# A recurrence of 576 steps before the main loop: its matrix products, and the products of zeros between them, split over TensorE's four column groups

## The chip, the cores and the metric

The kernel runs on one core of a Trainium2 chip. The metric is the device time of one execution in microseconds (us). The engines are named as in the profile: PE is TensorE's products, PEld TensorE's weight loads (they overlap the products), DVE is VectorE, ACT is ScalarE, POOL is GpSimd, SP is the engine that issues most transfers. L683 is line 683 of the kernel before.

## What is computed

The input x has 4 images of 128 channels and 64 x 64 pixels. Four layers follow one another, each with a residual sum: an attention over neighbourhoods of 7 x 7 with sampled offsets; a recurrent layer; eight layers of a selective state-space model; and a mixture of 64 experts. The change touches the second. Cut to what matters, the reference there is:

```python
Wx = einsum('bti,hi->bth', x, W)            # then normalised over all b and t, times gamma, plus beta
def step(yt, wx_t):
    yt = sigmoid(wx_t + yt @ V.T)
    return yt, yt
_, ys = scan(step, zeros((B, H)), swapaxes(Wx, 0, 1))
```

B is 4, H is 128, and there are 4096 steps (the pixels of an image). Each step needs the one before it, so the steps are a chain: a product of the 128 x 128 matrix V with four columns, a sum, a sigmoid.

## The kernel before

**The stages.** `tile_kernel` calls `conv_layer` (the attention and the product with W, whose result goes to HBM as wx_d), makes a `Recurrence`, calls `mamba` (the state-space layers) and then `experts`. All order is written out by hand: instructions run on each engine in the order in which the program gives them.

**The recurrence.** `Recurrence.step(t)` and `Recurrence.tanh(t)` do one step for all four images. The sigmoid is computed as a tanh, with the constants folded into V (`vt`, halved) and into the input. Steps come in blocks of RT = 64. At the first step of a block, L678 puts the block's input, 64 x 4 columns, into a PSUM tile `p` by a product with the identity; each step then adds its product with `vt` into its own four columns of that tile (L683, `start=False`), and ACT takes the tanh of those four columns (L691) into `z`, which is the moving operand of the next step's product. `vt` is the stationary operand, so TensorE loads it as weights. The matrices are f32. In the middle of a block `load` fetches the next block's input (L664, L666) and ACT scales it (L667); at a block's end POOL makes y from z and adds x1 (L697, L698), and SP writes the result to HBM (L700).

**The lead.** The state-space layers work on chunks of 512 pixels, so they can begin when the recurrence is ahead by somewhat more than a chunk. `mamba` therefore runs the first PRE = 512 + 64 = 576 steps by themselves, in a loop of their own: `rec.step(t)`, one or two calls of `rec.busy`, `rec.tanh(t)`. The other 3520 steps are given out one by one between the instructions of the state-space layers, by the list STEPS.

**The products of zeros.** `rec.busy(out, n)` (L655) multiplies a 128 x 128 bf16 tile of zeros, `still`, with n x 128 columns of the same zeros, into a PSUM tile `idle` that nobody reads. It does no part of the computation; it keeps TensorE working. In the lead each step has one with n = NB = 4 (512 columns), and every second step one more with n = 2 (256 columns). They stand on TensorE behind the step's product and ahead of the next step's.

**Where column groups are used already.** A product with 32 columns of weights writes 32 of the 128 partitions of PSUM, and the four possible positions are the array's four column groups. The kernel has such products at L433 in the attention and at L1423, L1508 and L1543 in the experts: in each, four products that follow one another in the program go to the four groups.

Of the kernel before, what the change touches and what calls it, by code (L numbers as in the profile page):

```python
# [20 lines left out]
P = 128  # L21
# [25 lines left out]
TL = 512  # L47
# [562 lines left out]
class Recurrence:  # L610
# [56 lines left out]
        nc.scalar.activation(wx, wx, AF.Identity, scale=self.sc, bias=self.sh)  # L667
        self.got[n] = wx, x1

    def step(self, t):  # L670

        nc = self.nc
        n, k = divmod(t, RT)
        if k == 0:

            self.wx, self.x1 = self.got.pop(n)
            self.p = self.ps.tile([P, RT, B], F32, tag="p", name="p")
            nc.tensor.matmul(  # L678
                self.p, self.ops.ident, self.wx.rearrange("p b t -> p t b"), start=True, stop=False,
                skip_group_check=True,  # L680
            )
            self.z = self.w.tile([P, RT, B], F32, tag="z", name="z")
        nc.tensor.matmul(  # L683
            self.p[:, k, :], self.vt, self.before, start=False, stop=True, skip_group_check=True
        )

    def tanh(self, t):

# [58 lines left out]
def mamba(tc, ops, I, rec, x2_d, x3_d):  # L747
# [8 lines left out]
    nc = tc.nc  # L756
    NSLOT = NS // 2 * NH
    NB = TL // P
# [5 lines left out]
    with ExitStack() as ctx:  # L764
# [408 lines left out]
        def get(i):  # L1173
            return bodies[i] if 0 <= i < len(bodies) else None
# [34 lines left out]
        load(0)  # L1209
        idle = psf.tile([P, TL], F32, tag="f0", name="idle")  # L1210
        for t in range(PRE):
            rec.step(t)
            rec.busy(idle, NB)
            if t % 2:
                rec.busy(idle, NB // 2)
            rec.tanh(t)
        for s in bodies[0:3]:
            for what in ("fetch", "mean", "var", "rv", "rr", "first"):
# [2 lines left out]
        t = PRE  # L1221
        for i in range(-2, len(bodies) + 1):
            o, n, q = get(i), get(i + 1), get(i - 1)
# [364 lines left out]
@with_exitstack  # L1588
def tile_kernel(ctx: ExitStack, tc: tile.TileContext, I, out):
    nc = tc.nc  # L1590
    const = ctx.enter_context(tc.tile_pool(name="const", bufs=1))
    dram = ctx.enter_context(tc.tile_pool(name="scratch", bufs=1, space=DRAM))
    nc.scalar.preload_act_table_set(EXP_LN)
    ops = Ops(nc, const)
    stats = const.tile([P, B * NBLK, 6], F32, name="stats")
    gating_w = gating_weights(tc, const, ops, I)
    x1_d = dram.tile([P, B, L], F32, name="x1_d")
    x2_d = dram.tile([P, B, L], F32, name="x2_d")
    x3_d = dram.tile([P, B, L], F32, name="x3_d")
    wx_d = dram.tile([P, B, L], F32, name="wx_d")  # L1600

    with tc.manual_schedule():
        with ExitStack() as c:
            conv_layer(tc, ops, I, x1_d, wx_d, stats)
            rec = Recurrence(c, tc, ops, I, stats, wx_d, x1_d, x2_d)
            mamba(tc, ops, I, rec, x2_d, x3_d)
        experts(tc, ops, I, gating_w, x3_d, out)
# [90 lines left out]
```

## Time and profile before

| | us |
|---|---|
| median of three runs (14884.57 to 14900.8) | 14895.22 |
| the profiled execution | 14892.08 |
| its span, first to last instruction | 14890.3 |
| the lead's tanh, first to last start | 1506.0 to 1881.6 |
| PE busy over the span | 14160.7 (95%) |
| DVE busy | 12974.0 (87%) |
| POOL busy | 12589.8 (85%) |
| ACT busy | 10980.2 (74%) |

The profile is of one execution, 1.8 us longer than its span. The granted clock of TensorE was 0.984 of full speed on average; the trace lists it by stretches, and in the lead it was 1.00 throughout. A busy PE in this profile is not PE at its peak, since products are pipelined and their ends are modelled: PE is shown busy for 361.7 of the 370 us from 1510 to 1880, although it streams for less than half of that time. A product or a load is recorded with the time at which it starts; two loads of which the second starts before the first is over are no error of the view.

In the groups' lines, the first number after the bar is busy time in us, then comes the mean duration of one in ns, and after the second bar the idle time of the engine just before them and what ended it. `128*32 128x128` in a product's line means weights of 128 rows and 32 columns, and a moving operand of 128 partitions and 128 elements.

### The profile page before, as it was taken

The numbers are of one execution on the slowest core, as the hardware profiler recorded it, in microseconds if no ns is written. First come the engines' busy times: TensorE is split into PE (matmuls) and PEld (weight loads), VectorE is DVE, ScalarE is ACT, GpSimd is POOL, SyncE is SP. The second block draws the span as 40 slices with busy tenths as digits, with TensorE's granted clock in tenths as the row PEclk, the third lists the DMA queues.
The fourth block names the chain that finished last, engine by engine and source line by source line (L and its number), as shares of the span: only waits on it lengthen the run. The fifth ranks groups of instructions, "written<-read, shape, count | busy, mean of one in ns | idle before, by whom it ended". The sixth has DMA issues, their size and how long they took to land. (4 is left out here: it accounts for less than half of the span.)

```text
span 14890.3 us, 307789 instructions
## 1 busy us (share of the span) xinstructions
PE 14160.7 (95%) x124378; PEld 10821.2 (73%) x124378; DVE 12974.0 (87%) x16043; ACT 10980.2 (74%) x21400; POOL 12589.8 (85%) x5760
## 2 busy tenths in 40 slices
PE   7999989999999999999999999999999999999996
PEld 3444467777777777777777777777777777777775
DVE  8997079998999899999998999989999999989994
ACT  6887267777777777777777777777777777777773
POOL 5564079999999999999999999999999999999993
PEclk8999999999999999999999999999999999999998
DMA  0000034434443434343444344344434343434344
GB/s 23 26 26 23 29 122 144 144 136 148 142 147 135 152 137 150 132 151 138 149 142 144 137 149 142 138 145 145 146 136 151 138 149 133 154 131 145 133 146 184
DMA packets 600044, 1914.56 MB, mean 129 GB/s; under 512 B 347488, under 2 KB 347872, under 8 KB 434272
## 3 DMA queue, kind: packets, MB, share of 16 engines
q1 hardware_dynamic: 598480, 1894.60, 36.1%
q8 instruction: 984, 16.12, 0.4%
q14 instruction: 436, 3.57, 0.1%
q10 hardware_dynamic: 144, 0.26, 0.0%
HBM read 1823.10 MB, written 71.57 MB: 127 GB/s over the span
## 5 line engine op out<-in xcount | busy, mean ns | idle before, releaser
L1100 POOL TENSOR_TENSOR hs<-hs,Cb 128x2048 f32<-128x2048 f32 x2048 | 9300.9, 4543 | 749.0 <-DVE state L1092 562.3
L1075 DVE TENSOR_TENSOR_SCAN hs<-dA,state,dBx 128x512 f32<-128x512 f32 x7168 | 8808.2, 1267 | 700.2 <-PE dBx L1042 561.3
L1020 ACT ACTIVATE dA<-dt,A 128x512 f32<-128x512 f32 x7168 | 4730.4, 716 | 11.6 <-DVE hs L1075 5.5
L1104 PE MATMUL yT<-ident,hs 128*128 128x128 f32 x32768 | 4376.9, 277 | 30.4 <-POOL hs L1100 30.2
L1042 PE MATMUL dBx<-diag,dtxT 64*128 64x128 f32 x57344 | 4195.3, 283 | 27.1 <-DVE hs L1075 20.1
L1104 PEld LDWEIGHTS yT<-ident,hs 128*128 128x128 f32 x32768 | 3785.4, 147 | 433.6 <-issue 349.2
L1042 PEld LDWEIGHTS dBx<-diag,dtxT 64*128 64x128 f32 x57344 | 3509.4, 187 | 800.7 <-issue 741.3
L683 PEld LDWEIGHTS p<-z,vt 128*128 128x128 f32 x8192 | 1283.9, 189 | 881.8 <-ACT z L691 401.8
L691 ACT ACTIVATE z<-p 128x4 f32<-128x4 f32 x4096 | 702.3, 171 | 1396.6 <-PE p L683 1368.8
L683 PE MATMUL p<-z,vt 128*128 128x4 f32 x8192 | 1453.7, 248 | 107.1 <-ACT z L691 98.4
L1075 DVE TENSOR_TENSOR_SCAN hs<-dAp,state,hs 128x512 f32<-128x512 f32 x1024 | 1273.3, 1273 | 296.7 <-POOL hs L1063 296.7
L1063 POOL TENSOR_TENSOR hs<-Bb,dtx 128x512 f32<-128x512 f32 x1024 | 1284.9, 1280 | 0.0
L904 DVE SCALAR_TENSOR_TENSOR xc<-f,taps,xc 128x511 f32<-128x511 f32 (+2 forms) x1536 | 1115.8, 726 | 53.4 <-ACT z L691 49.3
L1020 ACT ACTIVATE dAp<-dt,A 128x512 f32<-128x512 f32 x1024 | 708.8, 692 | 491.6 <-DVE hs L1075 470.1
L279 DVE SCALAR_TENSOR_TENSOR acc<-qp,dww,acc 128x512 f32<-128x512 f32 x1184 | 892.4, 754 | 25.6
L979 POOL TENSOR_TENSOR dtx<-dt,xc 128x512 f32<-128x512 f32 x512 | 651.6, 1273 | 217.5 <-ACT dt L973 217.5
L293 POOL TENSOR_TENSOR off<-off,to 128x512 f32<-128x512 f32 x288 | 366.4, 1272 | 412.7 <-ACT to L291 400.0
L1020 ACT ACT_TABLE_LOAD x511 | 655.6, 1283 | 9.0
L898 ACT ACTIVATE xc<-f,taps 128x512 f32<-128x512 f32 x512 | 350.7, 685 | 414.7 <-PE f L895 281.1
L919 PE MATMUL f<-u,given 128*128 128x512 f32 x1024 | 600.6, 670 | 3.8 <-DVE xc L904 3.8
L847 PEld LDWEIGHTS f<-avg,sq 128*128 128x128 f32 x2048 | 257.0, 197 | 466.0 <-ACT sq L1148 466.0
L895 PE MATMUL f<-u,given 128*128 128x512 f32 x1024 | 567.0, 636 | 0.8 <-DVE u L868 0.8
(235 smaller groups left out, 15160.8 us busy)
## 6 DMA issues: line engine op xcount, KB each, us to landing
Cb<-c_d SPq DMA_DIRECT2D x1024, 1024.0 KB, 7.2
diag<-spare SPq DMA_DIRECT2D x256, 1792.0 KB, 8.8
Bb<-c_d SPq DMA_DIRECT2D x256, 512.0 KB, 4.8
given<-in_m_given_dram SPq DMA_DIRECT2D x64, 640.0 KB, 8.6
slab<-in_w_dram SPq DMA_DIRECT2D x60, 512.0 KB, 9.9
x<-x_d SPq DMA_DIRECT2D x96, 256.0 KB, 3.0
c_d<-dbl SPq DMA_DIRECT2D x512, 32.0 KB, 1.6
x_d<-x SPq DMA_DIRECT2D x63, 256.0 KB, 3.2
```

Source lines behind the costliest of these rows:

```text
L279: nc.vector.scalar_tensor_tensor(rows(to), x, dww[:, t : t + 1], rows(o.acc), ALU.mult, ALU.add)
L683: nc.tensor.matmul(self.p[:, k, :], self.vt, self.before, start=False, stop=True, skip_group_check=True)
L691: nc.scalar.activation(self.z[:, k, :], self.p[:, k, :], AF.Tanh, scale=0.5)
L904: nc.vector.scalar_tensor_tensor(x, o.v[h][:, : TL - k], taps[:, o.l, h, DC - 1 - k : DC - k], x, ALU.mult, ALU.add)
L919: nc.tensor.matmul(o.pz[h], o.given[:, at : at + P], o.u, start=True, stop=True)
L979: nc.gpsimd.tensor_tensor(to, blocks(o.dt[h]), blocks(o.xc[:, h, :]), ALU.mult)
L1020: nc.scalar.activation(o.dA[j][:, k, :], o.dt[h], AF.Exp, scale=A[:, o.l, h, n : n + 1])
L1042: nc.tensor.matmul(o.dBx[j][:, at : at + 64, :], o.dtxT[h][row, n, :], o.diag[row, n, :, 2 * sp : 2 * sp + 2], start=True, stop=True,)
L1063: nc.gpsimd.tensor_tensor(hs[:, k, :].rearrange("p (q n t) -> p q n t", n=NB, q=2), o.Bb[:, k, :].rearrange("p (q n t) -> p q n t", n=NB, ...
L1075: nc.vector.tensor_tensor_scan(hs[:, k, :], o.dA[j][:, k, :], hs[:, k, :] if sp == SP_B else o.dBx[j][:, :, k], state[:, o.l, o.b, h, s : ...
L1100: nc.gpsimd.tensor_tensor(hs, hs, o.Cb[f], ALU.mult)
L1104: nc.tensor.matmul(o.yT[:, n, :], x[:, n * P : (n + 1) * P], ops.ident, start=start and n == 0, stop=True, is_transpose=True, skip_group_c ...
```

## The change

In the lead, `step(t, 4)` gives four products in place of one: each takes 32 columns of `vt` as weights, the same four columns of z as the moving operand, and writes 32 partitions of `p`. The product with the identity at the start of a block (L678) stays whole. In place of `rec.busy` stands `busy_tiles`: four products of zeros with 512 columns each, with 32 columns of weights each, one for each column group; the additional 256 columns of every second step are left out. The steps outside the lead call `step(t)` with one tile, which is one product as before.

```diff
+    def busy_tiles(self, out):
+
+        for j in range(0, P, 32):
+            self.nc.tensor.matmul(
+                out[j : j + 32, :].rearrange("p (n t) -> p n t", n=TL // P), self.still[:, j : j + 32],
+                self.still.unsqueeze(1).to_broadcast([P, TL // P, P]), start=True, stop=True,
+            )
+
-    def step(self, t):
+    def step(self, t, tiles=1):
...
-        nc.tensor.matmul(
-            self.p[:, k, :], self.vt, self.before, start=False, stop=True, skip_group_check=True
-        )
+        m = P // tiles
+        for j in range(0, P, m):
+            nc.tensor.matmul(
+                self.p[j : j + m, k, :], self.vt[:, j : j + m], self.before, start=False, stop=True,
+                skip_group_check=True,
+            )
...
         for t in range(PRE):
-            rec.step(t)
-            rec.busy(idle, NB)
-            if t % 2:
-                rec.busy(idle, NB // 2)
+            rec.step(t, 4)
+            rec.busy_tiles(idle)
             rec.tanh(t)
```

In the order of the built instructions, a step of the lead has on TensorE four products, of which the first waits for ACT, and then four times a load of zeros and its product; before, it had one product that waits for ACT, and one or two times a load of zeros and its product. The other engines have the same instructions in the same order as before.

## The prediction

> **What bounds the kernel now.** I began with the page's busy shares by slice. In slice 5 (1489 to 1861 us) VectorE and GpSimd are all but idle, so whatever is running there runs alone. The list of waits of 1510 to 1880 us says what it is:
>
> ```profile
> engine line waited for: us in total, times, longest us
> ACT z L691 <- PE p L683: 269.2, 551, 1.4
> PEld p L683 <- ACT z L691: 176.3, 552, 0.4
> ```
>
> TensorE (PE; its weight loads are the row PEld) and ScalarE (ACT) wait for each other, about 550 times. This is a chain of steps with nothing beside it: a shorter step ends the stage sooner. The chain that ended last does not show it, because that view's pieces cover only the last 300 us. From the same stretch, the groups kept apart by shape (busy us, mean ns | idle before):
>
> ```profile
> L683 PE MATMUL p<-z,vt 128*128 128x4 f32 x1120 | 215.0, 262 | 8.3
> L683 PEld LDWEIGHTS p<-z,vt 128*128 128x128 f32 x1120 | 167.4, 188 | 179.9 <-ACT z L691 176.3 <-issue 3.6
> L655 PEld LDWEIGHTS <-still 128*128 128x128 bf16 x840 | 108.7, 153 | 0.0
> L691 ACT ACTIVATE z<-p 128x4 f32<-128x4 f32 x560 | 96.9, 173 | 269.2 <-PE p L683 269.2
> ```
>
> 560 tanh but 1120 loads and products: each f32 product is two passes, each with a weight load of its own. The timeline of one step:
>
> ```profile
> 1601.38 0.30 PEld L683 LDWEIGHTS p<-z,vt 128*128 128x128 f32 x2 [0.33 <-ACT z L691]
> 1601.38 0.39 PE L683 MATMUL p<-z,vt 128*128 128x4 f32 x2
> 1601.51 0.21 PEld L655 LDWEIGHTS <-still 128*128 128x128 bf16 x2
> 1601.62 0.48 PE L655 MATMUL idle<-still 128*128 128x512 bf16 x2
> 1601.80 0.17 ACT L691 ACTIVATE z<-p 128x4 f32<-128x4 f32 x1 [0.48 <-PE p L683]
> 1602.03 0.19 PEld L683 LDWEIGHTS p<-z,vt 128*128 128x128 f32 x1 [0.30 <-ACT z L691]
> ```
>
> A step takes 1602.03 - 1601.38 = 0.65 us; over the trace's single records it is 648 ns. Those records of a step, counted from its first load: second load at 108 ns, so one load of 128 columns takes about 107; second product at 134; zeros' product at 246; tanh from 423 to 596; next load at 648. A second load that starts at 108 is done at 215, and only then can the second product stream its 4 columns. So the step is 215 ns of loads, 208 from there to the tanh, 173 of tanh and 52 to the next load: 648. A third of it is loading weights that never change. The zeros stream from 246 to 460 (512 columns, 214 ns), in every second step to 567: they end 80 ns or more before the next load, off the path.
>
> **What four column groups cost here.** The kernel already has such products at L1423: 128 columns stream, each product with 32 columns of weights. The first loads and products of one burst, from the timeline:
>
> ```profile
> 14786.25 0.16 PEld L1423 LDWEIGHTS pp<-slab,pk 128*32 128x32 f32 x8 [0.17 <-issue]
> 14786.25 0.32 PE L1423 MATMUL pp<-slab,pk 128*32 128x128 f32 x4
> ```
>
> And windows over such bursts and over L1543's, which are of the same kind (busy us and count of PE, PEld, DVE, ACT, POOL, then the granted clock, which the trace lists in steps of 3.41 us):
>
> ```profile
> 14786.20:14794.20 8.00, 8.00 (x203) 6.45 (x205) 5.48 (x10) 2.26 (x4) 3.30 (x1) 1.00 0.01 3
> 14812.62:14816.03 3.41, 2.23 (x48) 1.19 (x38) 0.00 (x0) 0.00 (x0) 0.00 (x0) 1.00 1.03 419
> 14816.03:14819.45 3.42, 1.52 (x35) 0.95 (x33) 0.00 (x0) 0.00 (x0) 0.00 (x0) 1.00 1.02 413
> 14819.45:14822.86 3.41, 2.90 (x52) 2.31 (x56) 0.00 (x0) 0.00 (x0) 0.00 (x0) 0.50 1.03 420
> ```
>
> In the burst eight loads fit into 0.16 us: single records start at 0, 7, 14, 20 ns for the first pass and 29, 35, 42, 49 for the second. So a load of 32 columns takes 27 to 29 ns, and the groups follow one another at 7, side by side. The second pass's products start 133 ns after the first's: 107 of streaming and those 27.
>
> **Part 1, the step's products.** By these times the last group's second load starts at 49 and is done at 76, where it was 215: 139 ns less. What follows (208, 173, 52) stays, so the tanh starts at 284 and the next load at 509. PRE is 576 steps; in nine of them the new block's L678 comes first, its two products of 256 columns hide V's loads, and I count no gain. 567 x 139 ns = 79 us.
>
> A rule of the Trainium skill speaks against this. "TensorE: Matmul & The Clock Gate", section Back-to-back issue gap, puts a floor of about 25 ns from one product's start to the next, however few columns it has. Eight products of 4 columns would need 27 + 7 x 25 = 202 ns, 13 less than now and not 139, worth 7 us in all. The row has four products start within 0.32 - 0.30 = 0.02 us, 7 ns apart, when they lie in different column groups. I take the row, but its products are long: that short ones of one group also keep the pace is not shown.
>
> **Part 2, the zeros.** Per step one product of 512 columns, in every second step another of 256, becomes four of 512 with 32 columns of weights, one for each group. They are queued behind the step's products on TensorE and run while the tanh is awaited. Their loads come behind the products', so they can start at about 105 to 125 ns. From below: all four stream at once, 213 ns, ending near 340, 170 before the next load: nothing on the path. From above: bf16 groups take turns, 4 x 216 = 864 ns, ending near 967. No bf16 product in column groups is in the trace. The nearest row is L1508, f32, 512 columns, 32 columns of weights: its groups of four start 7 ns apart and repeat every 429 ns, which is also what one pass of an unsplit 512-column f32 product takes. I take the first. If the cover is gone, each ns of zeros beyond 509 - 105 = 404 costs one ns per step.
>
> **Part 3, instructions.** The build has 12 instructions per step on TensorE where there were 4 on average; in the trace's records, 8 loads and 8 products and 4 of each for zeros, 24 in 509 ns: 21 ns each. In the window at 14786 us above, 203 + 205 = 408 ran in 8.00 us, 19.6 each, in spite of waits for VectorE, for longer than any short queue could hide. I count nothing; were 27 ns the limit the step would be 648 again.
>
> **Part 4, the clock.** The zeros are what keeps TensorE busy enough for the full clock (1.00 all through this stage). Now they and the step's products stream (213 + 53 + 7) / 648 = 42% of the time; after, counted once for four groups, (213 + 7) / 509 = 43%, and the staggered starts add to it. The last three windows above show how column groups count: 48 products of 107 ns, four at a time, are 38% of a window, and the next was still granted 1.00; 35 products are 27%, and the next was granted 0.50. So I count nothing. At half clock (L1423's rounds of four take 213 ns there, 109 at full clock) the zeros would take 427 ns, the step some 575: still 73 below now.
>
> Changing between split and unsplit products at the nine L678 costs between nothing and one draining product (0.27 us) each way: 0 to 5 us. I take 0. No wait, DMA or other engine's work is added; the first of four products carries the wait for ACT, and behind it are only its own group.
>
> **Sum.** The profiled execution took 14892.1 us (span 14890.3). 14892.1 - 79 = 14813; the median of the runs is 3 us above it, so 14816 there.
>
> **The rivals.** (a) *The gain is halved.* If each of the four products reports its end by itself, the same skill page (section The cost: per-tile semaphore tail) has 26 ns for each: 3 x 26 = 79 off 139, 60 left, 34 us, 14861. Half clock gives about the same: 73 x 567 = 41, 14854. For it: no such short groups are in the trace. (b) *It hardly does what it says.* Short products in groups keep the 25 ns floor, or the instructions the 27: 0 to 7 us, 14890. Against it: the 7 ns starts and 19.6 ns above. (c) *Slower: the zeros take turns.* Products end at 105, zeros at 967, and the next step's products wait behind them on TensorE: 967 per step, 319 x 567 = 181 us more, 15076. It decides from 545 ns of zeros on (648 - 103), two and a half products in turn; two pairs in turn (432) would still gain. Against it: L1508's groups, whose f32 pass reads as many bytes per ns as bf16 does. For it: the zeros are loads and products written out singly, which no split product of the trace is.
>
> **How the numbers follow.** The gain as computed 0.62; halved (a) 0.13; hardly any (b) 0.08; slower, (c) or any mixture of it, 0.17. The range goes from 14795, where the tail behind the second product also shrinks by 35 ns, through (a) to (b)'s 14890; only (c) is left out. A measurement of this kernel can tell some 0.2% (30 us) from no change: faster 0.75, same 0.08, slower 0.17.
>
> **What would show it.** Right: tanh starts about 509 ns apart; loads of 128x32 at L693's products, eight starting within 50 ns; the zeros of four groups starting together and over before the next load; the stage from 1505 to 1886 us ending near 1807; the clock 1.00 in it; all later stages as long as before. Wrong: a tanh interval of 570 to 590 with clock 0.5 or with late tanh starts (a); zeros' starts 216 ns apart (c); loads of V that idle on "issue" (b).

## The result, and the profile after

| us | before | changed |
|---|---|---|
| median of 5 runs each | 14892.51 | 14829.48 |
| the profiled execution | 14892.08 | 14829.05 |
| its span | 14890.3 | 14827.2 |
| the lead, first to last tanh | 1506.0 to 1886.1: 380.1 | 1505.3 to 1826.1: 320.8 |

The ratio is 0.996, with a 95% interval from 0.9945 to 0.9974: 63 us less, where 79 were forecast. One number given earlier has to be corrected: the table ahead of the prediction ends the lead before at 1881.6 us. That counted seven semaphore records of ACT as tanh; the last of the 576 starts at 1886.1, which is what the prediction itself used.

The lead is 59.3 us shorter, it begins 0.7 us sooner, and the remaining 3 us lie in the 13 ms behind it, which is within what executions of one kernel differ by (the five of the changed kernel go from 14828.4 to 14838.2).

In the list of waits of 1510 to 1820 us the pair is the same as before. TensorE waits no less for each tanh, but ACT waits far less for the products:

```profile
ACT z L702 <- PE p L693: 210.5, 546, 1.5
PEld p L693 <- ACT z L702: 199.7, 547, 1.2
PEld p L693 <- issue: 6.7, 9, 0.8
```

210.5 us in 546 waits are 0.39 us each, where it was 0.49. The third line is new in this size: eight of its nine cases, 6.0 us, are the starts of blocks, where split loads now stand behind a whole product, and the ninth is a pause that comes up below. The groups by shape, from 1510 to 1800 us:

```profile
L673 PE MATMUL idle<-still 128*32 128x512 bf16 x2072 | 207.4, 381 | 0.0
L693 PE MATMUL p<-z,vt 128*32 128x4 f32 x4152 | 128.0, 183 | 31.0 <-ACT z L702 0.9 <-issue 0.6
L702 ACT ACTIVATE z<-p 128x4 f32<-128x4 f32 x518 | 89.5, 173 | 197.3 <-PE p L693 197.3
L693 PEld LDWEIGHTS p<-z,vt 128*32 128x32 f32 x4147 | 82.3, 108 | 193.0 <-ACT z L702 186.3 <-issue 6.7
```

Eight loads and eight products of 32 columns for each tanh, and four products of zeros. The tanh takes 173 ns as before. The timeline of one step:

```profile
1600.41 0.16 PEld L693 LDWEIGHTS p<-z,vt 128*32 128x32 f32 x8 [0.36 <-ACT z L702]
1600.41 0.24 PE L693 MATMUL p<-z,vt 128*32 128x4 f32 x8
1600.46 0.12 PEld L673 LDWEIGHTS <-still 128*32 128x32 bf16 x4
1600.49 0.40 PE L673 MATMUL idle<-still 128*32 128x512 bf16 x4
1600.72 0.17 ACT L702 ACTIVATE z<-p 128x4 f32<-128x4 f32 x1 [0.36 <-PE p L693]
...
1600.95 0.16 PEld L693 LDWEIGHTS p<-z,vt 128*32 128x32 f32 x8 [0.36 <-ACT z L702]
```

Eight loads again fit into 0.16 us, as those of L1423 did. The four zeros' products start together behind the step's and are shown as over at 1600.89, ahead of the next load. From the single records, counted from the first load: loads at 0, 6, 13, 20 and at 28, 35, 41, 48 ns, the last product at 74, the zeros at 86 to 106, the tanh at 313, the next load at 538. With 27 ns for a load, the last one is done at 75: the loads did what they should. But from there to the tanh it is 238 ns, not 208.

The sum of the lead: 567 steps x 110 ns (648 to 538) are 62.4 us less. Against it stand two pauses near the beginning (steps of 1366 and 1422 ns, 1.7 us), the eight steps that begin a block (1650 ns, before 1566: 0.7), and ten steps at half clock (580 ns: 0.4). That leaves 59.6, and 59.3 were measured.

### The profile page after: what moved, and what is told of

The parts are those of the page before. It is cut to its first block, busy times and chain, and to the rows that moved or that the text cites. A ratio compares the mean times of both kernels' runs of the same rounds, so it can differ in the third digit from the quotient of the medians.

```text
span 14827.2 us, 317581 instructions
## 1 busy us (share of the span) xinstructions
PE 14069.7 (95%) x129274; PEld 10727.6 (72%) x129274; DVE 12973.9 (88%) x16043; ACT 10979.3 (74%) x21400; POOL 12589.7 (85%) x5760
## 3 DMA queue, kind: packets, MB, share of 16 engines
q8 instruction: 1022, 16.74, 0.5%
## 5 line engine op out<-in xcount | busy, mean ns | idle before, releaser
L693 PEld LDWEIGHTS p<-z,vt 128*128 128x128 f32 (+1 forms) x11648 | 1203.2, 157 | 909.9 <-ACT z L702 426.7
L693 PE MATMUL p<-z,vt 128*128 128x4 f32 (+1 forms) x11648 | 1374.9, 221 | 132.1 <-ACT z L702 98.2
```

The lines of the kernel that those rows point to most:

```text
L693: nc.tensor.matmul(self.p[j : j + m, k, :], self.vt[:, j : j + m], self.before, start=False, stop=True, skip_group_check=True,)
```

## The experiments

In all of them only the lead's loop differs from the changed kernel; each is timed beside runs of the kernel before on the same chip. The question is which part of the change gives the 110 ns, and where the 30 ns stay.

### Steps split, zeros whole

```diff
             rec.step(t, 4)
-            rec.busy_tiles(idle)
+            rec.busy(idle, NB)
+            if t % 2:
+                rec.busy(idle, NB // 2)
```

> The steps of the lead are split over four column groups as in the changed kernel; the products of zeros are whole again, as before (512 columns, in every second step 256 more). Theory (the gain is the weights' loads, and the zeros only hold the clock): the loads still shrink by 139 ns, so a step stays near the changed kernel's 538 ns and the run near 14829 us. Rival (split and whole products do not overlap in the array, so that each change between them waits for the other kind to leave it): zeros start some 170 ns later, end at 475 or 582 ns, and the next loads wait again; the step is 645 ns or more, and the run is at 14890 us or above.

Measured: 14850.28 us, ratio 0.9971 (0.9961 to 0.9981). The steps alternate between 538 and 606 ns. One of the long ones and the short one behind it, from the timeline:

```profile
1650.25 0.16 PEld L693 LDWEIGHTS p<-z,vt 128*32 128x32 f32 x8 [0.27 <-ACT z L702]
1650.26 0.24 PE L693 MATMUL p<-z,vt 128*32 128x4 f32 x8
1650.43 0.11 PEld L655 LDWEIGHTS <-still 128*128 128x128 bf16 x2
1650.43 0.50 PE L655 MATMUL idle<-still 128*128 128x512 bf16 x2
1650.57 0.17 ACT L702 ACTIVATE z<-p 128x4 f32<-128x4 f32 x1 [0.36 <-PE p L693]
...
1650.86 0.16 PEld L693 LDWEIGHTS p<-z,vt 128*32 128x32 f32 x8 [0.32 <-ACT z L702]
...
1651.04 0.39 PE L655 MATMUL idle<-still 128*128 128x512 bf16 x1
...
1651.40 0.16 PEld L693 LDWEIGHTS p<-z,vt 128*32 128x32 f32 x8 [0.27 <-ACT z L702]
```

By the single records, the last split product starts at 1650.327 us and the zeros' load 100 ns later, at 1650.427 (in the changed kernel the split zeros' first product starts 12 ns behind the last split product). The second zeros' product starts at 1650.658 and streams for 107 ns, to 1650.765; the next step's loads start at 1650.860, another 95 ns later. So whole and split products do wait for each other: some 100 ns at each change, which is the rival's mechanism at half its price. Where one product of zeros stands behind the step, the wait is covered; where two stand there it costs 68 ns. Two thirds of the gain are in the split steps alone. The rest came with two changes at once, the zeros split and the second product of zeros dropped. The short steps here, with one whole product of zeros, are already as long as those of the changed kernel (538 ns), so dropping the second one would by itself account for the rest, and no part of it is seen to come from the split of the zeros; a run with the second one dropped and the first left whole was not made.

### Zeros split, steps whole

```diff
-            rec.step(t, 4)
+            rec.step(t)
             rec.busy_tiles(idle)
```

> Only the products of zeros are split; the step's product is whole, as before. Theory (the gain is the weights' loads): the step stays at 648 ns and the run at 14892 us, or it is slower if a change between split and whole products costs something in each step. Rival (the gain comes from the zeros, which are fewer and over sooner): most of the 63 us appear here, 14830 to 14845 us.

Measured: 15130.09 us, ratio 1.0157 (1.0142 to 1.0172). The gain does not come from the zeros. But neither theory had the size: the lead took 616.9 us. The first eight steps are 648 ns long, as expected, and then the clock goes (PE busy and count, granted clock, share of the transfer engines, GB/s):

```profile
1509.00:1514.00 5.00, 5.00 (x49) 1.00 1.00 408
1514.00:1520.00 6.00, 6.00 (x36) 0.51 0.90 279
1520.00:2125.00 605.00, 605.00 (x3386) 0.50 0.03 6
```

The lead begins at 1509 us. In 648 ns, 213 of zeros and 7 of the step's products stream: 34% of the time, below the 42% of before, and the clock fell at 1514.1 us, after the first 3.41 us window that held nothing but such steps. At half clock the step is 1067 ns, with all of it on the path: the second product starts at 237 ns, the zeros 283 later, the last of them 12 behind the first and 427 long, and the next load 108 behind its end. The clock does not come back within the lead, although the zeros' 427 ns and some 14 of the step's products are 41% of 1067 ns, the share that the changed kernel keeps the full clock with. In the changed kernel's few steps at half clock the same 441 ns are 76% of 580, and there it rose again. How large the share must be to raise a clock that has fallen is not shown beyond that.

### No zeros

```diff
             rec.step(t, 4)
-            rec.busy_tiles(idle)
```

> The changed kernel without any product of zeros in the lead's loop. Theory: the granted clock is 0.5 for the whole lead, and each step is as long as the few steps at half clock in the changed kernel, 580 ns instead of 538: 14829 + 567 x 0.042 = 14853 us, still below before. Rival (the 31 ns by which the tanh comes later behind the last product than before are the price of the zeros that stand right behind it): from the last product's start to the tanh it is then not 261 ns as at half clock with zeros but some 230, and the step is 550 ns, 14836 us.

Measured: 14855.36 us, ratio 0.9972 (0.9963 to 0.9982); the clock was 0.50 from 1510 to 1845 us, each step 580 ns:

```profile
1510.00:1845.00 335.00, 170.05 (x4504) 0.50 0.07 19
```

That is the theory's number, and the rival falls: the tanh comes 262 ns after the last product starts, as in the changed kernel's few steps at half clock with zeros (261). So the zeros behind the products do not delay them. The zeros are worth 42 ns per step, not more; even without any, the split step beats the kernel before.

### Zeros in one group

```diff
-        for j in range(0, P, 32):
+        for j in range(0, 32, 32):
```

> The changed kernel with one product of zeros per step, in the first column group alone, instead of four. If the clock's monitor counts the time in which any group streams: 1.00, the step at 538 ns, 14829 us. If it counts the share of the array: the zeros are a quarter, the clock is 0.5, the step is 580 ns and the run 14853 us. If the later tanh is the price of four zeros' products behind the step's, the tanh comes up to 30 ns sooner than in the changed kernel at the same clock.

Measured: 14822.95 us, ratio 0.9955 (0.9941 to 0.997). The step is 538 ns, and the clock is 1.00 throughout:

```profile
1510.00:1820.00 310.00, 265.83 (x5055) 1.00 0.08 21
```

A quarter of the array is enough: time in which any group streams is 213 + 7 of 538 ns, 41%. Counted by the share of the array it would be (213 / 4 + 7) / 538 = 11%, far below the 34% at which the clock fell with all four groups. So it is the time of any group that orders these runs, not the share of the array. The tanh again comes 240 ns after the last product: not one of the 30 ns belongs to the zeros of the other three groups. The pauses of the changed kernel's beginning are absent.

### Two groups, and one alone

```diff
-            rec.step(t, 4)
+            rec.step(t, 2)
             rec.busy_tiles(idle)
```

> The lead's step as two products of 64 columns of weights on two halves of the array; the zeros as in the changed kernel. The weights' loads should take 53 ns instead of 27, the last one done some 120 ns after the step's first instead of 76 (four groups) or 215 (whole). What is open is the 31 ns by which the tanh comes later behind the last load than before (239 ns, before 208). Theory 1 (products on a part of the array report 31 ns later, whatever their number): tanh 359 ns after the first load, step 584 ns. Theory 2 (each further group adds some 10 ns): 338 ns, step 563. Theory 3 (the two passes of one group follow each other too closely, 53 ns, and the second waits behind the first on its way out; here they are 80 apart): 328 to 335 ns, step 553 to 560. If zeros of 32 columns of weights and products of 64 exclude each other in the array, as whole and split ones did, 100 ns are added between the two kinds, and the zeros' end (some 540 ns) with another 95 delays the next step: 635 ns. Run 14829 + 567 x (step - 538): 14841 to 14884 us.

Measured: 14834.59 us, ratio 0.9962 (0.9948 to 0.9976), step 558 ns. One step from the timeline:

```profile
1650.00 0.29 PE L693 MATMUL p<-z,vt 128*64 128x4 f32 x4
...
1650.21 0.40 PE L673 MATMUL idle<-still 128*32 128x512 bf16 x4
...
1650.56 0.20 PEld L693 LDWEIGHTS p<-z,vt 128*64 128x64 f32 x4 [0.24 <-ACT z L702]
```

By the single records the zeros' first product starts 129 ns behind the step's last product, where it starts 12 behind it in the changed kernel: products of 64 and of 32 columns of weights wait for each other too. It costs nothing here, because the zeros then stream until 440 ns after the first load (the expectation had 540) and the next load comes at 558. Theory 1 is out. The last load is done at 115 ns and the tanh comes at 334, which both theory 2 (115 + 208 + 10 = 333) and theory 3 allow. And with only the last of the four groups' products left:

```diff
-        for j in range(0, P, m):
+        for j in (range(0, P, m) if tiles == 1 else (P - m,)):
```

> The lead's step is one product of 32 columns of weights in the last column group; the other three are left out, so 96 of the 128 channels of the recurrence get no product with V in the lead. Zeros as in the changed kernel. The two loads should take 54 ns. Theory 1 (products on a part of the array report 31 ns later): tanh 54 + 239 = 293 ns after the first load, step 518. Theory 2 (each further group adds some 10 ns): 54 + 208 = 262, step 487. Theory 3 (the two passes of one group follow too closely): as theory 1, 518 ns. Together with the run of two groups the three are told apart. Run 14817 us for 518 ns, 14800 us for 487.

Measured: 14805.18 us, ratio 0.9941 (0.9921 to 0.996), from two runs, step 488 ns. One step of it from the timeline:

```profile
1650.64 0.11 PEld L693 LDWEIGHTS p<-z,vt 128*32 128x32 f32 x1 [0.33 <-ACT z L702]
1650.64 0.19 PE L693 MATMUL p<-z,vt 128*32 128x4 f32 x1
1650.65 0.10 PEld L673 LDWEIGHTS <-still 128*32 128x32 bf16 x3
1650.65 0.40 PE L673 MATMUL idle<-still 128*32 128x512 bf16 x3
1650.67 0.11 PEld L693 LDWEIGHTS p<-z,vt 128*32 128x32 f32 x1
1650.69 0.17 PE L693 MATMUL p<-z,vt 128*32 128x4 f32 x1
...
1650.90 0.17 ACT L702 ACTIVATE z<-p 128x4 f32<-128x4 f32 x1 [0.32 <-PE p L693]
```

Its tanh starts 210 ns after its second product. Theory 1 and theory 3 both needed 518 ns and fall. The time from the last load's end to the tanh, from the single records of each kernel:

| groups per step | whole array (before) | one of 32 | two of 64 | four of 32 |
|---|---|---|---|---|
| last load done, ns | 215 | 56 | 115 | 75 |
| tanh starts, ns | 423 | 264 | 334 | 313 |
| between | 208 | 208 | 219 | 238 |
| step | 648 | 488 | 558 | 538 |

The first row is the start of the last load plus the time of one load (107, 27 or 54 ns). The row "between" shows no cost for a part of the array as such, and about 10 ns for each further group: theory 2. Two groups lose to four because their loads are twice as long. Note also that in the run of one group three zeros' products start ahead of the step's own second pass. So the order of the program, which the text on the kernel before takes as the order on each engine, holds here for the first pass of each product: a second pass can be overtaken by later products of other groups.

### Zeros three times

```diff
-            rec.busy_tiles(idle)
+            for _ in range(3):
+                rec.busy_tiles(idle)
```

> The changed kernel with its four products of zeros three times in each step. Theory (each ns of zeros behind the 404 ns of cover costs one): they end some 106 + 642 = 748 ns after the first load, and the step is 748 to 770 ns instead of 538: the run is at 14950 to 14960 us. Rival (the next step's products can pass the zeros that stand ahead of them, as a column group's loads can): no change, 14829 us.

Measured: 14929.36 us, ratio 1.0024 (1.0015 to 1.0034), step 704 ns; slower than before. The rival falls, and the theory is 44 to 66 ns too high. The step's loads do pass the zeros:

```profile
1650.10 0.32 PEld L693 LDWEIGHTS p<-z,vt 128*32 128x32 f32 x8
1650.29 0.22 PE L693 MATMUL p<-z,vt 128*32 128x4 f32 x8
```

They start at 1650.10, when the tanh (1649.88 and 0.17 long) is ready, while the last zeros still stream; only the products wait, until 1650.29. So a step takes the zeros' 642 ns and 62 more, and by this working zeros begin to cost from 538 - 62 = 476 ns on, not from 404; between 213 and 642 ns nothing was measured.

### The better of two, again

> The kernel with the zeros in one column group alone again, beside the changed kernel on the same chip. If four zeros' products and loads per step cost more than they are worth (24 weight loads and products per step to be fetched and issued, against 18), this one is 3 to 8 us below the changed kernel: 14822 to 14826 us. If its earlier advantage was scatter, the two agree within 2 us.

> The changed kernel again, for the comparison: 14829 us, the lead's first to last tanh 321 us, with two pauses of some 0.85 us near its beginning in which TensorE waits for nothing that the profile shows.

Measured side by side: zeros in one group 14825.22 us (14821.0 to 14831.9), ratio to before 0.9956 (0.9942 to 0.9969); changed kernel 14827.57 us (14818.3 to 14843.8), ratio 0.996 (0.9948 to 0.9973). The two are the same by time: the 2.4 us between the medians, which lie between the two expectations, are less than either's spread. By the traces the lead is 318.5 us long with one group, in both of its runs, and 320.8 and 320.9 with four. The lead's 2.3 us are mostly the two pauses, which came back in the second run of the changed kernel (steps of 1541 and 1672 ns, at the same two steps). In the first run of it, one looks like this:

```profile
1510.40 0.14 PEld L693 LDWEIGHTS p<-z,vt 128*32 128x32 f32 x4 [0.36 <-ACT z L702]
1510.40 0.23 PE L693 MATMUL p<-z,vt 128*32 128x4 f32 x4
1511.26 0.11 PEld L693 LDWEIGHTS p<-z,vt 128*32 128x32 f32 x2 [0.72 <-issue]
```

In the middle of a step, between two groups' products, TensorE waits for nothing that the profile shows. By the profile's page, the instruction queue q8 carries 16.12 MB before and 16.74 after; in the trace its blocks of 16 KB follow one another every 3.5 to 7 us at the beginning of the changed lead, where they were 18 to 25 us apart. At 1511 us the transfer engines are still filled with the data that is loaded for the next stage (about 400 GB/s). That these pauses are code that comes late is a guess. For it speaks that the run with zeros three times (40 loads and products per step) has longer ones near the beginning too, 1.9 and 2.5 us, and that the runs with whole zeros or with zeros in one group have none there. It was not tried by itself.

## Why the prediction was right, and where its size was off

**What bounds.** Right: the lead was a chain of one product and one tanh with nothing beside it, and what its steps lost the kernel lost, 59.3 of 63 us in the lead itself.

**Part 1, the loads.** Right in mechanism and in its own number: the last load is done at 75 ns (76 was worked out from L1423), 140 less. The floor of about 25 ns between products' starts, which the Trainium skill states ("TensorE: Matmul & The Clock Gate", section Back-to-back issue gap), would have left the gain at an estimated 7 us. It does not hold across column groups in this trace, and the measurement decides: the short products start 6 to 7 ns apart in different groups and 53 ns apart within one.

**"What follows (208, 173, 52) stays"** is the term that was mis-sized. 173 and 52 stayed; 208 became 238. By the runs with one, two and four groups it is the number of groups that costs, some 10 ns for each after the first. 567 x 30 ns = 17 us of the 79 were lost to it, which is the difference between the 79 forecast and the 62 of the sum above. What makes it so (the ends of several groups reported in turn, or results that leave the array in turn) stays open. In the trace a single report of the four products ends each step, so the 26 ns for each report that stood behind rival (a) are not what is seen, though rival (a)'s direction was.

**The steps that begin a block** were counted at no gain; they lost 84 ns each, 0.7 us in all. The 0 to 5 us given for changing between whole and split products contained it.

**Part 2, the zeros.** Right: bf16 zeros in four groups start 20 ns apart at most and stream together; with 213 ns each they end at 320 ns, 340 was said. The cover is larger than given (476 ns, not 404): 29 ns of it because the step is longer than forecast, the rest because the zeros start at 86 ns rather than 105 and the next loads pass them.

**Part 3, instructions.** Nearly right: the sustained rate is no limit, 24 loads and products in 538 ns run all through the lead. The two pauses of 0.8 us were not foreseen.

**Part 4, the clock.** Right in its way of counting (any group's time counts once). That 575 ns was said for the steps at half clock and 580 measured is luck: half clock was to add 66 ns to 509, and it added 42 to 538. The clock is nearer to falling than the text says: whole steps with these same zeros lost it within eight steps at 34%. Steps of two groups, at 39% (213 + 7 of 558 ns), kept it all through the lead, and the changed kernel, at 41%, kept it but for two windows of 3.4 us right behind the pauses (its lead in two stretches, with columns as above):

```profile
1510.00:1520.00 10.00, 8.02 (x188) 0.83 0.62 197
1520.00:1820.00 300.00, 268.42 (x6508) 0.99 0.06 13
```

**The rivals.** (b) and (c) did not occur. Of (c), the point was real: with zeros of 642 ns the kernel is slower than before.

## What to carry to other kernels

When a small product stands in a serial chain, look at its weight load, not at its columns: split over four column groups, the two passes' loads of the same 128 columns were done after 75 ns rather than 215, and the chain shortens by that difference less some 10 ns for each group after the first. Where other products stand between those of the chain, count about 100 ns for each change between whole and split ones, and see whether the wait in the chain covers it: with one whole product of zeros it did, with two it cost 68 ns. And before thinning out work that holds the clock, work out its share of the new step's time: shortening the step and thinning the zeros went together here, and with the zeros thinned and the step left long the kernel was 1.6% slower.

## What the runs showed of the hardware that was not expected

- One column group's zeros hold the clock at 1.00 as well as four groups' do, at 213 + 7 of 538 ns; 34% of the time (whole steps, 648 ns) did not, and the clock then stayed at 0.50 for 600 us, although at half speed the zeros and products were 41% of each step.
- In four groups the tanh came 30 ns later behind the last load than in one group or in the whole array, in two groups 11 ns later.
- A group's products overtake the second pass of an earlier f32 product in another group: zeros of three groups at 1650.65 us, ahead of the step's second pass at 1650.69, whose product the program has before them.
- Products of 64 and of 32 columns of weights did not overlap in the run of two groups: the zeros started 129 ns behind the step's last product, 12 ns where both had 32.
